# Attention and mixture-of-experts block: token lists by pair of experts written to DRAM sequence by sequence, an earlier table load, and products of the identity between the first transposes

## The chip, the cores and the metric

The kernel runs on one core of one Trainium2 chip. A time is the device time of one execution in microseconds (us). The figure that counts is the median of the runs; beside it one execution was taken by the hardware profiler, and its durations are those that the text works with. The core's engines are called PE (matrix products, with PEld for its weight loads), DVE (vector work), ACT (activations, copies), POOL (the general engine, which also issues indirect DMAs) and SP (which issues most DMAs).

## The reference, cut to what matters

The input is x, 16 sequences (B) of 512 tokens (S) of 256 numbers (D), in float32.

```
xn = layernorm(x)
q, k = elu(xn@Wq + bq) + 1, elu(xn@Wk + bk) + 1      # 16 heads of 16
v  = xn@Wv + bv
kv = sum over tokens of k (outer) v                  # per head
attn = (q @ kv) / max(q . sum(k), 1e-6) @ Wo + bo

shared = swiglu(xn@w_in.T) @ w_out.T                 # hidden 512
group  = argmax(softmax(xn@wg.T + gb))               # 2 groups of 4 experts
p      = softmax(expert logits within the group) * p_group
w_se   = the two largest p of a token, at their experts, else 0
h      = swiglu(xn@w1.T)
routed = sum over e of (h * w_se[:, e]) @ w2[e].T
out = x + attn + shared + routed
```

A token uses two of the four experts of one group, so there are 6 pairs in each group, 12 in all (`NP`). The 8192 tokens are sorted by pair, so that a tile of 128 tokens needs only the two weight matrices of its pair.

## The kernel before, in words

Tokens stand in 64 tiles of 128 (`TT`), four to a sequence (`NT`). The program has three stretches.

*The head.* `first` (L300 to L382) is written out by hand and pinned in program order: statistics of the first sequence's four tiles on DVE (`measure`, L320), square root on ACT (`scale`, L325), the normalised `xn` on DVE (L328), two transposes to a tile on PE (`place`, `pt`, L335), a copy back on ACT (L338), then the products for keys and router logits (`keys`, `pk`, L342) and for queries. The weights of the router (`we`, `wg`) and `wk` are loaded from ACT's queue (L143 to L145), ahead of the activation at L147 that brings in the square root's table. x is loaded from SP's queue (L110): the first sequence tile by tile, the next as a whole, and the third, `xs[2]`, last of the head's loads.

*The loop over sequences.* Each stage b makes the front of b+1 (residual L390, projections L412 and L423, feature map L397 to L402, routing L446 to L515), sums over b (`summarize` L689, `key_sum` of b+1 at L679), the attention's normaliser of b+1 (`attend`, L743 to L750, the chain through `rz`), the two hidden layers of b (`hidden_rows` L595 for the experts, `hidden` L621 for the shared part, both by a scheme of seven products for eight, whose sums and differences run on DVE at L574 to L584), the values (`pvk` L708, `vk` L717 and L722), their mixture with Wo (`pm` L731) and the outputs (`po` L768, in `gather`, which adds them to the residual at L777). Rows of 770 numbers (hidden state, residual and two weights) go to `h_d` in DRAM. Routing leaves two things for the sorting: `hot`, for each token a one-hot row of 12 over the pairs, and `ahead_of`, per partition a running count over tiles of the tokens of each pair (POOL, L515).

*The tiles.* With the tokens sorted, 75 tiles (`TILES`) are walked: the class `Tiles` gathers rows of `h_d` by indirect DMA (`rows`, L943, with the list `source`), transposes them (`turn`, L964 to L976), multiplies by two experts (`sums`, L993 to L1003) and scatters the result into the output (L1006, with the list `goal`). 67 tiles always run, the rest under a condition on `filled`.

Between loop and tiles stands `order` (L806 to L923), a generator. It is stepped by `between` from within `hidden_rows` and `gather` of the last two sequences. Its first part adds up the counts over partitions with two float32 products `pc` (L813, L815) and works out each token's slot among the sorted places. Then, for 8 groups of 8 tiles, `marks` makes one-hot rows of slot and tile on DVE (L877, L882, L886, L890) and `add` accumulates 64 bf16 products of them in `pi` (L894), which ends as a table of 128 places by 75 tiles with the number of the token in each. `source` and `goal` are read off it (L908 to L923).

The framework's scheduler sets the order on each engine, by priority and by what is ready, except where the kernel pins it. PSUM has two pools: `ps_mm` with six buffers and `ps_y` with two. SP issues its DMAs in program order[...].

Of the kernel before, what the change touches and what calls it, by code (L numbers as in the profile page):

```python
# [21 lines left out]
def block_kernel(  # L22
# [55 lines left out]
    TG = 8  # L78
    TR = 5
    assert TT % TG == 0  # L80
# [10 lines left out]

    h_d = dram.tile([TT * P, ROW], FP, name="h_d")

# [12 lines left out]
    def load_x(b, pieces=1):  # L106
        xt = x_all[:, b % 2]
        n = NT // pieces
        for i in range(pieces):
            tc.keep_in_program_order(nc.sync.dma_start(  # L110
                out=xt[:, ts(i, n), :], in_=x[b, ts(i, n * P), :].rearrange("(t p) d -> p t d", p=P)
            ))
        return xt
# [16 lines left out]
    xs = {0: load_x(0, NT)}  # L130
    KR = D + E + G
    wkr_sb = wp.tile([P, KD, KR], FP)

# [8 lines left out]

    nc.scalar.dma_start(out=wkr_sb[:, :, D : D + E], in_=we.rearrange("(p c) e -> p c e", p=P))  # L143
    nc.scalar.dma_start(out=wkr_sb[:, :, D + E : KR], in_=wg.rearrange("(p c) e -> p c e", p=P))
# [50 lines left out]
    def load_expert(i):  # L195
# [21 lines left out]
    before = const.tile([P, P], FP)  # L217
    nc.gpsimd.affine_select(
        out=before, in_=ones, pattern=[[1, P]],
# [4 lines left out]
    for j in range(EG):  # L224
        nc.gpsimd.memset(place[:, :, j : j + 1], float(j))
    BF = mybir.dt.bfloat16
    count = const.tile([P, P], BF)
    nc.gpsimd.iota(count, pattern=[[1, P]], base=0, channel_multiplier=0,
                   allow_small_or_imprecise_dtypes=True)
    number = const.tile([P, TT], BF)  # L230
    nc.gpsimd.iota(number, pattern=[[1, TT]], base=1, channel_multiplier=0,
                   allow_small_or_imprecise_dtypes=True)
    row = const.tile([P, 1], FP)
    nc.gpsimd.iota(row, pattern=[[0, 1]], base=0, channel_multiplier=1,
# [65 lines left out]
    def first():  # L300
# [57 lines left out]

        for t in range(NT):
            measure(0, t)  # L360
            scale(0, t, 1)
            if t:
                place(0, t - 1)
        keys(0)
# [152 lines left out]
    def between(b, n):  # L517

        if b + 2 >= B:
            for _ in range(n or 0):  # L520
                next(steps_of_order)
# [68 lines left out]
    def hidden_rows(b, xs7, then):  # L590

        rows = {}

        def product(to, u, i, start, stop):
            tc.keep_in_program_order(nc.tensor.matmul(  # L595
                to, lhsT=xs7[i][:, ts(u, P)], rhs=w1_in[W7[i]], start=start, stop=stop,
                skip_group_check=True,
            ))

        def room(u, half):  # L600
            rows[u, half] = work.tile([P, HID], FP, tag="hr", name=f"hr_{b}_{u}_{half}", bufs=4)
            return rows[u, half]

        def done(u, half, silu, product):
            nc.sync.dma_start(out=h_d[ts(b * NT + 2 * half + u, P), 0:HID], in_=rows[u, half])

        seven(f"phr_{b}", product, lambda a: a, room, done, lambda n: between(b, then(n)))
# [89 lines left out]
    def small_sums(b, shape, name):  # L697

        if b + 1 == B:
            return ps_y.tile(shape, FP, tag="py", name=f"{name}_{b}"), tc.keep_in_program_order  # L700
        return ps_mm.tile(shape, FP, tag="mm", name=f"{name}_{b}"), lambda step: step
# [25 lines left out]
    def mix(b, vk):  # L727
# [7 lines left out]
        with tc.high_priority() if b + 1 == B else nullcontext():  # L735
            nc.scalar.copy(kvo, pm)
# [22 lines left out]
    def outputs(b, t, qT, kvo, hs):  # L759
# [6 lines left out]
        parts += [(qT[:, c, ts(t, P)], kvo[:, c, :]) for c in range(KD)]  # L766
        for i, (a, w) in enumerate(parts):
# [3 lines left out]
    def gather(b, res, qT, kvo, hs, placed, then):  # L771

        for t in range(NT):
# [5 lines left out]
            between(b, then(t))  # L779
# [26 lines left out]
    def order():  # L806

        I32, U32 = mybir.dt.int32, mybir.dt.uint32
        total = keep.tile([P, NP], FP)
        nc.vector.tensor_copy(total, ahead_of[:, TT, :])  # L810
        pc = ps_mm.tile([P, 2 * NP], FP, tag="mm", name="pc")
        tc.keep_in_program_order(
            nc.tensor.matmul(pc[:, 0:NP], lhsT=before, rhs=total, start=True, stop=True)  # L813
        )
        nc.tensor.matmul(pc[:, NP:], lhsT=ones, rhs=total, start=True, stop=True)  # L815
        pcs = keep.tile([P, 2 * NP], FP)
# [3 lines left out]
        nc.vector.tensor_scalar(ci, pcs[:, NP:], float(P - 1), None, ALU.add)  # L820
# [5 lines left out]
        nc.vector.tensor_copy(runs[0][:, PAD:], ci)  # L826
        for i, d in enumerate((1, 2, 4, 8)):
# [3 lines left out]

        off = keep.tile([P, NP], FP)
        nc.vector.tensor_tensor(off, pcs[:, 0:NP], starts, ALU.add)
        sl = one.tile([P, TT, NP], FP, tag="low", name="sl")
        nc.vector.tensor_tensor(
            sl, ahead_of[:, 0:TT, :], off.unsqueeze(1).to_broadcast([P, TT, NP]), ALU.add
        )
        nc.vector.tensor_tensor(sl, sl, hot, ALU.mult)
        slot = keep.tile([P, TT], I32)
        slf = keep.tile([P, TT], FP)  # L840
        nc.vector.tensor_reduce(slf, sl, AX.X, ALU.add)
        nc.vector.tensor_copy(slot, slf)
        part = keep.tile([P, 2, TT], I32)
        nc.vector.tensor_scalar(part[:, 0, :], slot, P - 1, None, ALU.bitwise_and)
        nc.vector.tensor_scalar(part[:, 1, :], slot, 7, None, ALU.arith_shift_right)
        place_of = keep.tile([P, 2, TT], BF)
        nc.vector.tensor_copy(place_of, part)
# [12 lines left out]
        nc.vector.tensor_copy(where, of)  # L860
        yield


        pi = ps_y.tile([P, 2 * TILES], FP, tag="py", name="pi")

        los = x_all.rearrange("p b t d -> p (b t d)").bitcast(BF).rearrange("p (n t j) -> p n t j", t=TG, j=P)
        his = [
            a[:, B % 2].rearrange("p t d -> p (t d)").bitcast(BF)[:, 0 : TG * 2 * TILES].rearrange(
                "p (t i n) -> p t i n", t=TG, i=2
            )  # L870
            for a in (qq_all, kk_all, xn_all)
        ]

        def marks(g):
            row_of, tile_of = (place_of[:, i, ts(g, TG)].unsqueeze(2) for i in range(2))
            lo, hi = los[:, g % 4], his[g % 3]
            nc.vector.tensor_tensor(  # L877
                lo, count.unsqueeze(1).to_broadcast([P, TG, P]), row_of.to_broadcast([P, TG, P]),
                ALU.is_equal,
            )  # L880
            at_tile = one.tile([P, TG, TILES], BF, tag="at_tile", name=f"at_tile_{g}")
            nc.vector.tensor_tensor(  # L882
                at_tile, count[:, 0:TILES].unsqueeze(1).to_broadcast([P, TG, TILES]),
                tile_of.to_broadcast([P, TG, TILES]), ALU.is_equal,
            )
            nc.vector.tensor_tensor(  # L886
                hi[:, :, 0, :], at_tile,
                number[:, ts(g, TG)].unsqueeze(2).to_broadcast([P, TG, TILES]), ALU.mult,
            )
            nc.vector.tensor_scalar(hi[:, :, 1, :], at_tile, row, None, ALU.mult)  # L890

        def add(g):
            for t in range(TG):
                tc.keep_in_program_order(nc.tensor.matmul(  # L894
                    pi, lhsT=los[:, g % 4, t, :], rhs=his[g % 3][:, t].rearrange("p i n -> p (i n)"),
                    start=(g + t == 0), stop=(g * TG + t == TT - 1),
                ))


        for g in range(TT // TG + 2):  # L900
            if g > 1:
                add(g - 2)
                yield
            if g < TT // TG:
                marks(g)
                yield
        pis = keep.tile([P, 2, TILES], FP)
        nc.vector.tensor_copy(pis.rearrange("p i n -> p (i n)"), pi)  # L908
        free = keep.tile([P, TILES], FP)
        nc.vector.tensor_scalar(free, pis[:, 0, :], 0.0, float(2 * TT * P), ALU.is_equal, ALU.mult)  # L910
        tok = keep.tile([P, TILES], FP)
        nc.vector.scalar_tensor_tensor(
            tok, pis[:, 0, :], float(P), pis[:, 1, :], ALU.mult, ALU.add
        )
# [6 lines left out]
        nc.vector.tensor_scalar(source, tok, float(-P), 0.0, ALU.add, ALU.max)  # L921
        goal = keep.tile([P, TILES], U32)
        nc.vector.scalar_tensor_tensor(goal, tok, float(-P), free, ALU.add, ALU.add)  # L923
# [109 lines left out]
    xs[2] = load_x(2)  # L1033
    for b in range(B):
# [4 lines left out]
        if b + 2 == B:  # L1039
# [4 lines left out]
            steps_of_order = order()  # L1044
        if b + 1 == B:
            sums7 = token_sums(b, xnT)
            hidden_rows(b, sums7, {2: 2, 6: 2, 9: 2, 13: 2}.get)
# [3 lines left out]
            *lists, filled = next(steps_of_order)  # L1051
# [11 lines left out]
        elif b + 1 < B:  # L1063
            sums7 = token_sums(b, xnT)
            hidden_rows(b, sums7, {9: 1}.get)
# [5 lines left out]
        if b + 2 == B:  # L1071
            next(steps_of_order)
# [3 lines left out]
        if b + 1 < B:  # L1076
# [13 lines left out]
        if b + 2 == B:  # L1090
            next(steps_of_order)
# [5 lines left out]
        else:  # L1097
            gather(b, res, qT, kvo, hs, normed[b + 2][2]() if b + 2 < B else None, {0: 2, 1: 2, 3: 2}.get)
# [66 lines left out]
```

## Time and profile before

| | us |
|---|---|
| median of 3 runs | 1040.03 (1039.69 to 1040.49) |
| the profiled execution | 1033.23 |
| its span | 1031.5 |
| PE busy | 1004.9 (97%) |
| DVE busy | 779.4 (76%) |
| ACT busy | 488.1 (47%) |
| POOL busy | 254.8 (25%) |

The span is the time from the first to the last instruction that the profiler saw. An engine's busy time counts its instructions, not the time it stands before a semaphore. In a row of the timeline come start, duration, engine and line, operation, what is written and read, shapes, and in brackets the idle time before it with the instruction that ended that idle time. A row with x4 holds four instructions in sequence. The stage of one sequence takes some 46.5 us in the middle of the loop; the head ends, and the second sequence begins, near 74 us; the outputs of the last sequence end at 789.8, and after them come the tiles.

### The profile page before, as it was taken

Reading aid. Unit: us, or ns where it says so; the run is one execution under the profiler, and the core shown is the slowest. Engines: PE = TensorE matmul, PEld = TensorE weight load, DVE = VectorE, ACT = ScalarE, POOL = GpSimd, SP = SyncE. Lnnn points to the kernel's source line nnn. Section 1 sums busy time; section 2 is a strip of 40 time slices with the busy share of each in tenths; the row PEclk is TensorE's granted clock in tenths of the full one; section 3 lists DMA queues with packets and bytes.
Section 4 is the critical chain, followed back from the end, with each engine's and each line's share of the span. In section 5 each row is a group of like instructions: output and inputs, shape, how many; then the busy total and the mean of one; then the engine's idle time right before and its main releaser. Section 6 shows DMA issues by size and latency. Waiting matters only on the chain. (4 is left out here: it accounts for less than half of the span.)

```text
span 1031.5 us, 12407 instructions
## 1 busy us (share of the span) xinstructions
PE 1004.9 (97%) x3704; PEld 681.7 (66%) x3704; DVE 779.4 (76%) x1974; ACT 488.1 (47%) x893; POOL 254.8 (25%) x359
## 2 busy tenths in 40 slices
PE   7999999999999999999999999999899999999996
PEld 5466868677786868686777768686667344444442
DVE  5978687878778787878787877868975776666663
ACT  3525353535445253535343534425136576766671
POOL 5302020111202021110202020201012766555652
PEclk9999999999999999999999999999999999999999
DMA  7063534525152522314141313221235755555440
GB/s 220 16 177 107 141 104 101 147 59 154 51 163 54 161 84 81 122 42 143 37 128 56 110 55 123 72 77 61 62 110 146 225 172 153 147 156 157 150 147 30
DMA packets 130339, 116.08 MB, mean 113 GB/s; under 512 B 72637, under 2 KB 114109, under 8 KB 130272
## 3 DMA queue, kind: packets, MB, share of 16 engines
q1 hardware_dynamic: 120064, 77.43, 25.7%
q0 software_dynamic: 9392, 37.58, 12.2%
q8 instruction: 31, 0.51, 0.2%
q10 hardware_dynamic: 816, 0.27, 0.2%
q14 instruction: 36, 0.29, 0.1%
HBM read 65.36 MB, written 50.27 MB: 112 GB/s over the span
## 5 line engine op out<-in xcount | busy, mean ns | idle before, releaser
L993 PE MATMUL py<-w_sb,hT 128*128 x536 | 230.7, 592 | 1.7 <-DVE hT L976 1.6
L993 PEld LDWEIGHTS py<-w_sb,hT 128*128 128x128 f32 x536 | 101.7, 190 | 130.1 <-issue 129.1
L768 PE MATMUL po<-wout_sb,hs_all 128*128 128x256 f32 x480 | 116.6, 380 | 1.4 <-DVE hs_all L580 1.4
L390 POOL TENSOR_TENSOR res<-x_all,bo_sb 128x256 f32<-128x256 f32 x64 | 48.5, 792 | 274.4 <-DMA h_d<-res 203.4
L768 PEld LDWEIGHTS po<-wout_sb,hs_all 128*128 128x128 f32 x480 | 89.2, 190 | 15.1 <-DVE hs_all L580 3.4
L1006 POOL DMA_INDIRECT out<-y,goal x67 | 67.8, 1012 | 76.3 <-DVE y L1003 65.3
L676 POOL TENSOR_TENSOR k<-kk_all 128x512 f32<-128x512 f32 x16 | 20.9, 1307 | 258.3 <-DVE sm L458 247.7
L777 DVE TENSOR_TENSOR res<-po,res 128x256 f32<-128x256 f32 x60 | 25.4, 424 | 76.6 <-PE po L768 76.5
L398 ACT ACTIVATE km<-km 128x1024 f32<-128x1024 f32 x16 | 16.9, 1057 | 138.7 <-DVE km L397 134.4
L595 PE MATMUL phr_w<-w_sb,ss 128*128 128x512 f32 x120 | 61.5, 594 | 2.2 <-DVE ss L538 1.9
L768 PE MATMUL po<-kvo,qT 128*128 128x256 f32 x240 | 61.7, 383 | 0.0
L621 PE MATMUL phs_w<-ss,win_sb 128*128 128x256 f32 x240 | 61.6, 379 | 0.0
L621 PE MATMUL phs_t<-xnT,win_sb 128*128 128x256 f32 x240 | 61.6, 379 | 0.0
L595 PE MATMUL phr_t<-w_sb,xnT 128*128 128x512 f32 x120 | 61.3, 593 | 0.0
L595 PE MATMUL phr_t<-w_sb,ss 128*128 128x512 f32 x120 | 59.4, 597 | 0.0
L621 PE MATMUL phs_t<-ss,win_sb 128*128 128x256 f32 x240 | 59.1, 379 | 0.0
L689 PE MATMUL pxk<-kk_all,xn_all 128*128 128x256 f32 x256 | 58.0, 379 | 0.0
L412 PE MATMUL pk<-wkr_sb,xnT 128*128 128x266 f32 x240 | 57.2, 387 | 0.0
L423 PE MATMUL pq<-w_sb,xnT 128*128 128x256 f32 x240 | 54.2, 379 | 0.0
L689 PEld LDWEIGHTS pxk<-kk_all,xn_all 128*128 128x128 f32 x256 | 48.5, 190 | 6.7 <-issue 0.2
L964 ACT COPY hb<-qq_all 32x256 f32<-32x256 f32 x108 | 43.4, 402 | 17.1 <-DMA qq_all<-h_d,source 9.7
L412 PEld LDWEIGHTS pk<-wkr_sb,xnT 128*128 128x128 f32 x240 | 45.4, 190 | 8.0
(216 smaller groups left out, 1966.0 us busy)
## 6 DMA issues: line engine op xcount, KB each, us to landing
h_d<-hr SPq DMA_DIRECT2D x64, 256.0 KB, 2.5
q_d<-qq_all SPq DMA_DIRECT2D x16, 512.0 KB, 2.8
qb<-q_d SPq DMA_DIRECT2D x64, 128.0 KB, 3.1
w_sb<-in_w SPq DMA_DIRECT2D x64, 128.0 KB, 3.5
h_d<-res SPq DMA_DIRECT2D x60, 129.0 KB, 1.9
x_all<-in_x SPq DMA_DIRECT2D x15, 512.0 KB, 4.8
xn_d<-xn_all SPq DMA_DIRECT2D x14, 512.0 KB, 3.9
xb<-xn_d SPq DMA_DIRECT2D x56, 128.0 KB, 2.8
```

What stands on the lines that cost most here:

```text
L390: nc.gpsimd.tensor_tensor(res[:, t, 0:D], xt[:, t, :], bo_sb, ALU.add)
L412: nc.tensor.matmul(pk, lhsT=xnT[:, k, ts(t, P)], rhs=wkr_sb[:, k, :], start=(k == 0), stop=(k == KD - 1),)
L423: nc.tensor.matmul(pq[:, t, :], lhsT=xnT[:, k, ts(t2 + t, P)], rhs=wq_sb[:, k, :], start=(k == 0), stop=(k == KD - 1),)
L595: tc.keep_in_program_order(nc.tensor.matmul(to, lhsT=xs7[i][:, ts(u, P)], rhs=w1_in[W7[i]], start=start, stop=stop, skip_group_check=True,))
L621: tc.keep_in_program_order(nc.tensor.matmul(split(to)[:, f, :], lhsT=win_in[W7[i]][:, ts(2 * u + f, P)], rhs=xs7[i], start=start and f == ...
L676: nc.gpsimd.tensor_tensor(k2, kk[:, 0:2, :], kk[:, 2:4, :], ALU.add)
L689: nc.tensor.matmul(pxk[:, c, :], lhsT=xn[:, t, ts(c, P)], rhs=kk[:, t, :], start=(t == 0), stop=(t == NT - 1),)
L768: nc.tensor.matmul(po, lhsT=a, rhs=w, start=(i == 0), stop=(i == len(parts) - 1))
L777: nc.vector.tensor_tensor(res[:, t, 0:D], po, res[:, t, 0:D], ALU.add)
L964: nc.scalar.copy(there[ts(q, Q), a - near, 0:n, :], self.hg[ts(a, Q), 0:n, ts(q, W)])
L993: nc.tensor.matmul(py.rearrange("p j d -> p (j d)"), lhsT=self.hT[:, f, ts(j, P)], rhs=w2_sb[:, f, bass.ds(regs[i % TR], 2 * D)], start=(f ...
L1006: stored = nc.gpsimd.indirect_dma_start(out=out_rows, out_offset=bass.IndirectOffsetOnAxis(ap=self.goal[:, i : i + 1], axis=0), in_=y, in_ ...
```

## The change

Four parts.

1. *Lists by sequence.* After the routing of sequence b, `enlist(b)` works out the place of each of its 512 tokens within its pair: two bf16 products into `pr` (128x48), one of a triangular matrix with `hot`, one of ones with `ahead_of`; then four DVE operations, which add the start of the pair's list, mask, reduce to one number a token and tile, and turn it into an index `spot`. Four indirect DMAs from POOL write the tokens' numbers, 4 bytes each, into `lists_d` in DRAM, at a distance of 32 bytes. `clear_lists` first fills that array with a number that stands for "no token" (3.19 MB in seven DMAs from SP).
2. *`order`.* The one-hot groups, the 64 products and the slots are gone. One bf16 product `pc` gives the totals; a chain of small DVE operations gives, for each of the 75 tiles, the row of `lists_d` where it begins (`part`); one indirect DMA fetches those rows (`got`); a copy takes each eighth word (`tokens`), and a transposing product `pi` turns them into the layout of `source` and `goal`. It is no longer stepped from `hidden_rows` and `gather`; it starts after sequence 14's hidden layer. Within a list tokens now stand by tile and then by partition. An empty place gathers row 8191, where it was row 0, and is not scattered.
3. *Sequence 14.* Its values and mixture run within its hidden layer, as those of sequence 15 already did, and its outputs take the attention's part first.
4. *The head.* `we` and `wg` are loaded from SP's queue behind the second tile of x. Fifteen products of the identity with itself (`warm`) stand on PE: seven before the first transposes, two behind each of the first three pairs. Their result, `idle`, is not used.

The scheduler's order follows from these. On DVE in the head, the first statistics of the third sequence (L283, which need `xs[2]`) now stand ahead of five operations that stood before them: a first `ss`, two `ex`, and the additions of `kk_1_0` and its logits. In the loop, the pairs of `pr` products stand behind the key sums, and the four new DVE operations among the `rz` chain, ahead of the `hs` additions. The fifteen `idle` products, `pc` and `pi` use the pool `ps_y`.

The diff, cut to its core:

```diff
-    xs = {0: load_x(0, NT)}
+    def load_routers():
+        for w, at, n in ((we, D, E), (wg, D + E, G)):
+            tc.keep_in_program_order(nc.sync.dma_start(
+                out=wkr_sb[:, :, at : at + n], in_=w.rearrange("(p c) e -> p c e", p=P)
+            ))
+
+    xs = {0: load_x(0, NT, {1: load_routers})}
...
-    nc.scalar.dma_start(out=wkr_sb[:, :, D : D + E], in_=we.rearrange("(p c) e -> p c e", p=P))
-    nc.scalar.dma_start(out=wkr_sb[:, :, D + E : KR], in_=wg.rearrange("(p c) e -> p c e", p=P))
     nc.scalar.dma_start(out=wkr_sb[:, :, 0:D], in_=wk.rearrange("(p c) f -> p c f", p=P))
...
+        def warm(n):
+            for _ in range(n):
+                pin(nc.tensor.matmul(idle, lhsT=ident, rhs=ident, start=True, stop=True))
+
+        idle = ps_y.tile([P, P], FP, tag="py", name="idle")
+        warm(7)
         for t in range(NT):
             measure(0, t)
             scale(0, t, 1)
             if t:
                 place(0, t - 1)
+                warm(2)
...
+    def clear_lists():
+        free = work.tile([P, P * WORDS], U32, tag="blocks", name="free")
+        nc.gpsimd.memset(free, FREE)
+        R = lists_d.shape[0]
+        for r in range(0, R, P):
+            n = min(P, R - r)
+            nc.sync.dma_start(out=lists_d[r : r + n, :], in_=free[0:n, :])
...
+    def enlist(b):
+        pr = ps_y.tile([P, NT, NP], FP, tag="py", name=f"pr_{b}")
+        flat = pr.rearrange("p t c -> p (t c)")
+        mine = hot[:, ts(b, NT), :]
+        nc.tensor.matmul(flat, lhsT=before, rhs=mine.rearrange("p t c -> p (t c)"), start=True, stop=False)
+        nc.tensor.matmul(
+            flat, lhsT=ones_bf, rhs=ahead_of[:, ts(b, NT), :].rearrange("p t c -> p (t c)"),
+            start=False, stop=True,
+        )
+        rk = small.tile([P, NT, NP], FP, tag="rk", name=f"rk_{b}")
+        nc.vector.tensor_tensor(rk, pr, lists_at.unsqueeze(1).to_broadcast([P, NT, NP]), ALU.add)
+        nc.vector.tensor_tensor(rk, rk, mine, ALU.mult)
+        rf = small.tile([P, NT], FP, tag="rf", name=f"rf_{b}")
+        nc.vector.tensor_reduce(rf, rk, AX.X, ALU.add)
+        spot = small.tile([P, NT], U32, tag="spot", name=f"spot_{b}")
+        nc.vector.tensor_scalar(spot, rf, float(WORDS), None, ALU.mult)
+        for t in range(NT):
+            put = nc.gpsimd.indirect_dma_start(
+                out=entries,
+                out_offset=bass.IndirectOffsetOnAxis(ap=spot[:, t : t + 1], axis=0),
+                in_=ids[:, b * NT + t : b * NT + t + 1], in_offset=None,
+            )
+            tc.declare_no_dep(put.ins, group="lists", reason="every token has an entry of its own")
+            tc.add_to_no_dep_group("lists", put.ins)
...
-        if b + 1 == B:
+        if b + 2 >= B:
             return ps_y.tile(shape, FP, tag="py", name=f"{name}_{b}"), tc.keep_in_program_order
...
+        if b + 2 == B:
+            parts = parts[KH:] + parts[:KH]
...
     def order():
...
-        total = keep.tile([P, NP], FP)
-        nc.vector.tensor_copy(total, ahead_of[:, TT, :])
-        pc = ps_mm.tile([P, 2 * NP], FP, tag="mm", name="pc")
...
+        pc = ps_y.tile([P, NP], FP, tag="py", name="pc")
+        nc.tensor.matmul(pc, lhsT=ones_bf, rhs=ahead_of[:, TT, :], start=True, stop=True)
...
+        past = keep.tile([P, NP - 1], FP)
+        nc.vector.tensor_scalar(past, starts[:, 1:], row, None, ALU.is_le)
+        nc.vector.tensor_tensor(past, past, jump[:, 0 : NP - 1], ALU.mult)
+        begin = keep.tile([P, 1], FP)
+        nc.vector.tensor_reduce(begin, past, AX.X, ALU.add)
+        part = keep.tile([P, 1], U32)
+        nc.vector.tensor_scalar(part, begin, row, 1.0 / P, ALU.add, ALU.mult)
+        got = work.tile([P, P * WORDS], U32, tag="blocks", name="got")
+        nc.gpsimd.indirect_dma_start(
+            out=got[0:TILES, :], out_offset=None, in_=lists_d,
+            in_offset=bass.IndirectOffsetOnAxis(ap=part[0:TILES, :], axis=0),
+        )
+        tokens = keep.tile([P, P], FP)
+        nc.vector.tensor_copy(
+            tokens[0:TILES, :], got[0:TILES, :].rearrange("p (n w) -> p n w", w=WORDS)[:, :, 0]
+        )
         yield
-        pi = ps_y.tile([P, 2 * TILES], FP, tag="py", name="pi")
...
-        for g in range(TT // TG + 2):
-            if g > 1:
-                add(g - 2)
-                yield
-            if g < TT // TG:
-                marks(g)
-                yield
...
+        pi = ps_y.tile([P, TILES], FP, tag="py", name="pi")
+        nc.tensor.transpose(pi, tokens[0:TILES, :], ident[0:TILES, 0:TILES])
...
-        nc.vector.tensor_scalar(source, tok, float(-P), 0.0, ALU.add, ALU.max)
+        nc.vector.tensor_scalar(source, pi, float(TT * P - 1), None, ALU.min)
         goal = keep.tile([P, TILES], U32)
-        nc.vector.scalar_tensor_tensor(goal, tok, float(-P), free, ALU.add, ALU.add)
+        nc.vector.tensor_copy(goal, pi)
         yield source, goal, where, filled
...
     xs[2] = load_x(2)
+    clear_lists()
...
+        if b == 0:
+            enlist(0)
+        if b + 1 < B:
+            enlist(b + 1)
...
+            if b + 2 == B:
+                steps_of_order = order()
+                next(steps_of_order)
+            gather(b, res, qT, kvo, hs, normed[b + 2][2]() if b + 2 < B else None)
+            if b + 2 == B:
+                *lists, filled = next(steps_of_order)
```

## The prediction

> **What bounds the kernel now.** I read the busy shares first, then TensorE's waits, then the timeline of the stages that the change touches. From the page of the kernel before:
>
> ```profile
> span 1031.5 us, 12407 instructions
> PE 1004.9 (97%) x3704; PEld 681.7 (66%) x3704; DVE 779.4 (76%) x1974; ACT 488.1 (47%) x893; POOL 254.8 (25%) x359
> ...
> L1006 POOL DMA_INDIRECT out<-y,goal x67 | 67.8, 1012 | 76.3 <-DVE y L1003 65.3
> ```
>
> TensorE (PE) is busy for 97% of the span, so work taken off it, or a wait taken from it, shortens the span wherever PE sets the end. POOL is busy for a quarter. From TensorE's waits (for what: total, times, longest):
>
> ```profile
> PE pt L335 <- DVE xn_all L328: 7.5, 5, 5.3
> PE pm L731 <- DVE rz L748: 2.5, 1, 2.5
> PE phr_w L595 <- DVE ss L538: 1.9, 1, 1.9
> ...
> PE phs L663 <- DVE hr L651: 1.5, 1, 1.5
> ```
>
> The first is the start. The second and third belong to one place, the seam between sequence 14's stage and sequence 15's. Its timeline on PE (start, duration, operation; in brackets the idle time before it):
>
> ```profile
> 731.13 1.10 PE L731 MATMUL pm<-wo_sb,vk 128*128 128x256 f32 x4 [2.47 <-DVE rz L748]
> 735.49 0.69 PE L894 MATMUL pi<-qq_all,x_all 128*128 128x150 bf16 x8 [0.23 <-DVE qq_all L890]
> 738.22 0.59 PE L768 MATMUL po<-wout_sb,hs_all 128*128 128x256 f32 x2
> 738.65 0.70 PE L894 MATMUL pi<-kk_all,x_all 128*128 128x150 bf16 x8
> 739.19 1.50 PE L768 MATMUL po<-wout_sb,hs_all 128*128 128x256 f32 x6
> 744.52 1.06 PE L595 MATMUL phr_t<-w_sb,xnT 128*128 128x512 f32 x2
> 747.49 1.10 PE L595 MATMUL phr_w<-w_sb,ss 128*128 128x512 f32 x2 [1.91 <-DVE ss L538]
> ```
>
> The old list-building stands here: groups of one-hot comparisons (L877 to L890) keep DVE busy without a gap from 731 to 764.5, so `vk_14`, and then sequence 15's first sums, come late and PE waits. The x8 of the row at 738.65 takes up 0.54 us of PE (the next `po` starts at 739.19), 0.067 us a product.
>
> From there to the end it's PE again. The first row gathers start at 768.48, long before the first tile's product at 789.84, and the 24 products after it come every 0.43 us. A microsecond won near 735 reaches the end.
>
> In the head the bound changes hands:
>
> ```profile
> 8.97 1.98 PE L342 MATMUL pk<-wkr_sb,xnT 128*128 128x266 f32 x4
> 20.48 3.76 PE L412 MATMUL pk<-wkr_sb,xnT 128*128 128x266 f32 x16
> 24.78 0.43 DVE L283 BATCH_NORM_STATS2 st<-x_all 128x6 f32<-128x256 f32 x1 [2.48 <-DMA x_all<-in_x]
> 64.36 1.13 PE L731 MATMUL pm<-wo_sb,vk 128*128 128x256 f32 x4
> ```
>
> One size of product costs 0.49 us at 9 us and 0.235 us at 20 us: PE starts at half rate (the granted-clock column reads 1.00 in both, so only durations show it). DVE then stands 2.48 us for the third sequence's x, whose DMA the SP queue issues at 20.03. From 26.2 to 64 DVE has no idle time worth the name (29.87 of 30 us between 30 and 60), and `vk_0`, its last piece, ends at 64.31, just ahead of `pm`. So DVE's work behind 24.78 sets when PE leaves the first sequence.
>
> **Step 1, the old lists go (seam).** Removed from PE: 64 products of 0.067, 4.27 us; their wait, 0.2; the two fp32 products `pc` at 711, about 0.5; the waits for `vk` (2.47), for `ss` (1.91) and for `hr` (0.33), since what held DVE there, the marks, no longer exists. Sum 9.7 us off the path that sets the end.
>
> **Step 2, two `pr` products per sequence.** 32 bf16 products of 48 columns, each with a 128x128 weight load. Those of sequences 0 and 1 stand in the DVE-bound head; 28 stand in PE-bound stages. No row has their shape. Low end: two `pi` products with their loads, 0.13 us a pair. High end: the old `pc` pair (fp32, 12 columns), 0.25. They're bf16 like `pi`, but each change between fp32 and bf16 work leaves less to overlap, as at `pc`, so I take 0.2: 14 pairs, 2.8 us (1.8 to 3.5).
>
> **Step 3, lists by sequence on DVE and POOL.** DVE gets four small operations per sequence. By the nearest rows (L478 128x24 0.20, L510 reduction 0.19, L748 0.20) these are 0.7 to 0.8 us, behind `rz` (L743 to L750) and ahead of the `hs` additions. At 293.5 to 296.4 DVE waits 0.34, 0.44 and 0.42 us there, 1.2 in all, so this cover holds it: 0. Without the cover, 14 x 0.75 is 10.5 us. POOL gets 64 scatters of 128 entries of 4 bytes. By the L1006 row one costs POOL 1.01 us plus 0.30 between two, so 5.3 us per sequence of 46.5 on an engine that's three quarters idle. Queued behind them is only the next sequence's doubling of k (L676), some 10 us later. Nobody waits for the landing until the single gather `got` at the end: 0.
>
> A rule speaks against this step. The Trainium skill, "SBUF — State Buffer", section "Who interferes with whom", says that VectorE in a 2-port mode and GpSimd lock each other out for a whole instruction. The trace agrees that something of the kind exists: L467, 0.65 us usually, takes 1.02 while POOL runs L676. By the row of L943 (gathers of 0.95 to 1.04 us at 768 to 775, beside `vk` and `hs` operations at their usual 0.42 and 0.69) a scatter costs DVE nothing. By the rule a plain copy or tensor_scalar that meets one could wait up to about 1 us. Most operations near the scatters read two tensors or PSUM, so I go by the row and keep the rule for a rival.
>
> **Step 4, clearing the lists.** Seven SP DMAs, 3.19 MB, behind x[2]. SP issues nothing between 20.45 and 42.01, and at the 404 GB/s seen at 14 us they need 8 us: hidden, 0. Had they to share with the first q writes at 50, it would be up to 1 us.
>
> **Step 5, the new order at the seam.** A chain of some 16 small DVE operations starts after `phs_14` (about 728) and is interleaved with `hs` additions: about 6 us. Then one gather of 75 rows, 1 us of issue and 2.5 to 3.9 us to land (3.9 is the median of the row gathers), and a strided copy: tokens at 738 to 739.5. PE reaches the transposing product `pi` after four `po`, at about 739.1. So a wait of 0 to 2 us, taken as 0.5. Behind it on PE the whole of `phr_15` is queued. `pi` itself 0.3 and `pc` 0.1.
>
> **Step 6, the head.** The router weights move from ACT's queue to SP's, so ACT's table load (2.81, 1.28 us) starts 1.3 us earlier and the first `xn` (4.72) comes some 0.5 us earlier. Fifteen identity products keep PE at work before its first need. Cold `pk` records cost 4 x 0.255 + 5 x 0.19 = 1.9 us more than warm ones. The Trainium skill, "TensorE: Matmul & The Clock Gate", Part 1 (the HAM clock gate), says full rate comes after about 3.4 us of sustained work; with products from 2.6 us it would be there by 9, and all 1.9 us would go. By the trace, PE began at 5.28, worked in snatches, and was fast only at 13.2, 8 us later; from 2.6 that gives 10.6, and perhaps 1.2 of it goes. By neither is it worth anything at the end, since what follows still meets the wait for x[2] at 24.78. That load is issued behind two more SP DMAs (0.63 each): 0 to 1.3 later, taken as 0.6. And the new DVE order puts its statistics ahead of five operations which used to fill time before the wait (a first `ss`, 0.33; two `ex`, 0.18; `kk_1_0`, 0.33; `lg`, 0.10), so 0.94 us lands behind it, and eight list operations of sequences 0 and 1 add 0.9. Head: +2.4 us, from 0 to +4.
>
> **Sum.** -9.7 + 2.8 + 0.5 + 0.4 + 2.4 = -3.6. The profiled execution took 1033.23 (span 1031.5 and 1.7 around it), so 1029.6. The runs' median is 1040.03, 6.8 above it; carried along, the forecast is 1036.4.
>
> **Rivals.** B, full gain: the head is neutral because the ACT and clock gains carry through, and `pr` costs its low end. Then -9.7 + 1.8 + 0.9 to -7 or more, with a PE start that gains 1 to 2 it's -8.5: about 1031.5. For it: PE-bound stages have no other limit. Against it: the DVE stretch from 26 to 64.
>
> C, nothing measurable (0.2%, 2.1 us, is about what a measurement of this kernel can tell from no change): the token chain is 2 us late, the head +4, `pr` 3.5: -9.7 + 3.5 + 2.4 + 4 = +0.2, with milder terms about -0.5, so 1039.5. For it: three waits each have a cause ahead of them.
>
> D, slower: the scatters hold DVE, by the port rule. Place: between `rz` and the `hs` additions in each of 14 sequences. Cover there is 1.2 us, of which the list operations use 0.75, so a hold shows from 0.45 us per sequence and outweighs the 3.6 from 0.7. One hold of 1 us gives 14 x 0.55 - 3.6 = +4: 1044; two give 14 x 1.55 - 3.6 = +18: 1058. Against it: the L943 row.
>
> **How the numbers follow.** Forecast 0.45, B 0.2, C 0.15, D 0.2. The forecast's own range is 1033 to 1038.5. The range must hold C and the mild end of D: 1031 to 1044. Faster by over 0.2% (below 1038): B and most of the forecast, 0.6. Same: C and the forecast's upper end, 0.19. Slower: D and a little of C, 0.21.
>
> **What would show it.** PE's waits no longer list `pm` for DVE at 731 nor `phr_w` for `ss`; `phr_15` starts about 9 us sooner against `phs_14`'s end. DVE's `rz` and `hs` rows keep their means (1.22, 0.69). `pr` pairs stand 0.13 to 0.25 us apart. `pm_0` starts at 66 to 67 rather than 64.36; if it starts at or before 64, B holds. If the stretch from one sequence to the next grows beyond 46.5 us plus 0.2, D holds. The forecast is wrong above all if tokens come after 741, or if a stage that was PE-bound gains a wait on DVE.

## The result, and the profile after

The changed kernel is slower: 1045.79 us (median, 1044.67 to 1046.42) against 1040.03, a ratio of 1.0051 (95% interval 1.004 to 1.0062). The forecast was 1036.4, so it has the wrong sign. The changed kernel's page:

```profile
span 1044.7 us, 12545 instructions
PE 1009.7 (97%) x3696; PEld 685.3 (66%) x3696; DVE 756.2 (72%) x2000; ACT 487.8 (47%) x893; POOL 330.4 (32%) x426
...
L568 POOL DMA_INDIRECT lists_d<-ids,spot x64 | 74.2, 1160 | 184.4 <-DVE spot L566 158.0
L1008 POOL DMA_INDIRECT out<-y,goal x67 | 68.0, 1015 | 82.7 <-DVE y L1005 72.1
```

DVE has 23 us less to do, POOL 76 more, and the span is longer. TensorE's waits in the changed kernel (for what: total, times, longest):

```profile
PE py L995 <- DVE hT L978: 5.2, 1, 5.2
PE pr L555 <- DVE ksb L735: 5.1, 1, 5.1
PE idle L375 <- POOL ident masks.py:199: 2.6, 1, 2.6
PE pt L348 <- DVE xn_all L341: 2.4, 1, 2.4
PE pxk L743 <- DVE sm L479: 1.5, 1, 1.5
```

The waits of the seam (`pm` for `rz`, `phr_w` for `ss`) are gone, as forecast. In their place stands one at 52 us that no step of the forecast held: `pr` waiting for the copy of a key sum. The first row, among the tiles, isn't the change's: a second trace of the kernel before has it too, with 4.7 us. Of the traces behind this text some have one such wait of 4.5 to 5.2 us and tiles of 239 to 240 us, the others only short ones (at most 2.4 us) and tiles of 233 to 235 us, whichever kernel it is. The kernel before ran in 1040 us in most groups of runs and in 1033 in one, and the traces of that group all lack the wait; what decides it was not found. So below a time is compared with the kernel before run beside it, and stages with the second trace of before, which has the wait. By stages, in us:

| stage | before, second trace | changed | difference | forecast |
|---|---|---|---|---|
| head, to the first key product of sequence 2 | 73.74 | 82.81 | +9.1 | +2.4 |
| 13 stages, to the same of sequence 15 | 618.1 | 619.5 | +1.4 | +2.6 |
| seam and last sequence, to the first tile's product | 98.5 | 87.3 | -11.2 | -8.6 |
| tiles, to the last scatter | 239.6 | 239.9 | +0.3 | 0 |
| after the last scatter | 8.0 | 15.2 | +7.3 | 0 |
| span | 1037.9 | 1044.7 | +6.8 | -3.6 |

So the gain is there, and more than its size; it is lost again at two places, in the head and behind the last instruction that computes anything. The head of the changed kernel, on TensorE and with one row of DVE (the copy `ksb`):

```profile
48.46 0.19 PE L555 MATMUL pr<-hot,before 128*128 128x48 bf16 x1
48.49 0.18 PE L556 MATMUL pr<-ahead_of,ones_bf 128*128 128x48 bf16 x1
...
50.43 1.02 PE L717 MATMUL phs<-xnT,w_sb 128*128 128x512 f32 x2
51.29 1.02 PE L717 MATMUL phs<-xnT,win_sb 128*128 128x512 f32 x2
56.92 0.41 DVE L735 COPY ksb<-pks 128x256 f32<-128x256 f32 x1
57.39 0.20 PE L555 MATMUL pr<-hot,before 128*128 128x48 bf16 x1 [5.07 <-DVE ksb L735]
57.41 0.21 PE L556 MATMUL pr<-ahead_of,ones_bf 128*128 128x48 bf16 x1
57.45 3.76 PE L717 MATMUL phs<-xnT,win_sb 128*128 128x512 f32 x4
61.00 1.91 PE L717 MATMUL phs<-xnT,w_sb 128*128 128x512 f32 x2
62.71 2.90 PE L717 MATMUL phs<-xnT,win_sb 128*128 128x512 f32 x6
```

The second `pr` waits 5.07 us, and behind the wait a `phs` product takes 0.89 us from start to start (four from 57.45 to 61.00), where it took 0.43 ahead of it (two from 50.43 to 51.29): TensorE has fallen back to half rate. The granted clock is 0.50 from 57.4 to 62.7 and 1.00 ahead of the wait. The six products take 5.26 us instead of 2.58, so 2.7 us more. The Trainium skill ("TensorE: Matmul & The Clock Gate", Part 1) has the clock halved after an idle window of about 3.4 us, until about as long a stretch of sustained work. This wait fits the first half of that; the slow stretch behind it is longer, 5.3 us. And 3.4 us is no sharp bound here: in the seam of the second trace of before, a wait of 2.48 us was enough (granted clock 0.61 behind it), and in the first trace one of 2.47 was not (1.00).

And the end. POOL's last drain, in the rows of the program's closing line, of the second trace of before and of the changed kernel (durations in ns, shortest, median and longest, then first and last start in us):

```profile
L1161 POOLq DRAIN  x3: 51/103/3418, 1033.6 to 1037.6; - x3
```

```profile
L1167 POOLq DRAIN  x3: 51/103/8727, 1035.1 to 1044.4; - x3
```

The long one is 3.418 us before and 8.727 after. The last instructions of the other engines come only when it is done.

### The profile page after: what moved, and what is told of

Read it like the earlier page. It is cut to its first block, busy times and chain, and to the rows that moved or that the text cites. A ratio compares the mean times of both kernels' runs of the same rounds, so it can differ in the third digit from the quotient of the medians.

```text
span 1044.7 us, 12545 instructions
## 1 busy us (share of the span) xinstructions
PE 1009.7 (97%) x3696; PEld 685.3 (66%) x3696; DVE 756.2 (72%) x2000; ACT 487.8 (47%) x893; POOL 330.4 (32%) x426
## 4 chain that ended last, share of the span: by engine, by line
PE 81%; DVE 9%; DMA 3%; issue 3%; ACT 1%; SPq 1%; another core or an unknown queue 1%; POOL 0%; POOLq 0%; DVEq 0%; ACTq 0%
PE py L995 20%; PE po L824 14%; PE phr_t L649 9%; PE phs_t L675 7%; PE pk L433 5%; PE pxk L743 5%; PE pq L444 5%; PE phr_w L649 4%; PE phs_w L675 3%; PE phr_l L649 2%; PE phs_l L675 2%; PE pm L785 1%; PE phs L717 1%; DMA x_all<-in_x 1%; DMA w_sb<-in_w 1%
## 5 line engine op out<-in xcount | busy, mean ns | idle before, releaser
L568 POOL DMA_INDIRECT lists_d<-ids,spot x64 | 74.2, 1160 | 184.4 <-DVE spot L566 158.0
L419 ACT ACTIVATE km<-km 128x1024 f32<-128x1024 f32 x16 | 16.9, 1058 | 140.9 <-DVE km L418 136.6
```

The costliest lines, as they stand in the source:

```text
L568: put = nc.gpsimd.indirect_dma_start(out=entries, out_offset=bass.IndirectOffsetOnAxis(ap=spot[:, t : t + 1], axis=0), in_=ids[:, b * NT + ...
```

## The experiments

### Second traces

Both kernels unchanged.

> The kernel before, unchanged, for a second trace. The first profiled execution (1033.2 us) lies 6.8 under the median of the runs (1040.0). Theory A, that it was a lucky execution: this one takes about 1040, and the 7 us show as one more stall among the tiles or as a later end of TensorE's sequencer after the last product. Theory B, that the profiler itself shortens it: again 1033.

> The changed kernel, unchanged, for a second trace. Its first trace reaches the first tile's product at 789.57 (before: 789.84) and then loses 13 us: 5.2 in one wait near 818, 2 at half clock behind it, and 7 after the last scatter. Theory A, that these come from the new order of tokens in the lists: the same wait at the same tile. Theory B, that they are how executions fall: another place or none, and a time anywhere from 1037 to 1046.

Before: 1039.65 us, span 1037.9, with a wait of 4.73 us for `hT` at 819 to 824, and a last drain of 3.418 us as in the first trace. Changed: 1044.88, span 1043.2, the same wait (4.67), drain 8.727 again, and the wait for `ksb` (3.5 us). Theory A of the first holds as to the wait, and not as to the end, which is the same in both traces of before. Of the second, both theories fall: the wait among the tiles is in both kernels, and the long end is not how an execution falls; it is in every trace of the changed kernel. The stages repeat well: the 13 stages took 618.1 us in both traces of before and 619.5 in both of the changed kernel.

### The list of sequence 0 made one stage later

Key sums and `pr` both take their PSUM buffers from `ps_y`, which has two. In stage 0 the key sum of sequence 1 holds one, the first `pr` gets the other, and the second must wait until DVE has copied the key sum out.

```diff
-        if b == 0:
-            enlist(0)
         if b + 1 < B:
             enlist(b + 1)
...
+            if b == 1:
+                enlist(0)
             if b + 2 == B:
                 steps_of_order = order()
```

> The changed kernel with the list of sequence 0 made in stage 1 instead of stage 0, so that the second PSUM pool's two buffers hold key sums 1 and one list product, not two. Theory A, that the second pr product waited 5.07 us for a buffer (until VectorE had copied key sum 1) and threw the clock back to half rate: the wait at 52 to 57 is gone, the second sequence's first keys start at 74 to 76 rather than 80.1, and the time falls by 4 to 6 us. Rival, that VectorE sets the end of the first sequence anyway: the wait moves to the mixture pm, and the time falls by less than 2.

1040.4 us beside 1040.03 for before: ratio 1.0004 (0.9995 to 1.0013), some 5 us under the changed kernel. The head of this kernel on TensorE:

```profile
47.62 0.19 PE L555 MATMUL pr<-hot,before 128*128 128x48 bf16 x1
48.37 0.18 PE L556 MATMUL pr<-ahead_of,ones_bf 128*128 128x48 bf16 x1 [0.56 <-POOL ahead_of L536]
...
51.12 2.74 PE L717 MATMUL phs<-xnT,win_sb 128*128 128x512 f32 x6
...
66.71 1.10 PE L785 MATMUL pm<-wo_sb,vk 128*128 128x256 f32 x4 [0.92 <-issue]
...
76.28 3.76 PE L433 MATMUL pk<-wkr_sb,xnT 128*128 128x266 f32 x16
```

The wait for `ksb` is gone and so is the half rate behind it (one of 0.56 us for the counts is left), and the first key product of sequence 2 starts at 76.28 instead of 82.81 (81.64 in the second trace of the changed kernel). Theory A holds. What is left is VectorE's again: `vk_0` ends at 66.61, and `pm` starts at 66.71, 2.35 to 2.57 us later than in the two traces of before.

### The head undone

```diff
-    xs = {0: load_x(0, NT, {1: load_routers})}
+    xs = {0: load_x(0, NT)}
...
+    nc.scalar.dma_start(out=wkr_sb[:, :, D : D + E], in_=we.rearrange("(p c) e -> p c e", p=P))
+    nc.scalar.dma_start(out=wkr_sb[:, :, D + E : KR], in_=wg.rearrange("(p c) e -> p c e", p=P))
...
-        warm(7)
...
-                warm(2)
```

> The changed kernel with the head undone: router weights on ACT's queue, no products of the identity. Theory A, that the two loads ahead of x tiles 3 and 4 and of the third sequence's x cost some 2 us at the wait for that x: the statistics of the third sequence start at 24.8 rather than 26.7, and the time falls by about 2. Rival, that the clock and table gains pay for it: the time rises by 0 to 2.

1043.21 us, ratio 1.0031 (1.0019 to 1.0042): some 2 us better than the changed kernel. But the statistics of the third sequence start at 26.54, no earlier than with the new head (26.67). The size came out as theory A had it and its mechanism didn't: the two loads are not what delays that x. This kernel keeps the wait for `ksb`, with 3.45 us, and its sequence 2 starts at 80.64, so part of its gain is a shorter wait and not the head undone. What the two loads do delay shows on DVE in the changed kernel:

```profile
5.79 0.41 DVE L341 TENSOR_SCALAR xn_all<-x_all,mv,rs 128x256 f32<-128x256 f32 x1
9.26 0.43 DVE L333 BATCH_NORM_STATS2 st<-x_all 128x6 f32<-128x256 f32 x1 [3.06 <-DMA x_all<-in_x]
```

DVE has to wait for the third tile of x until 9.26, where in the kernel before it takes that tile at 6.58 without a wait, so TensorE stands for 2.4 us after its products of the identity and starts its first keys at 11.72, at half rate again:

```profile
11.27 0.61 PE L375 MATMUL idle<-ident 128*128 128x128 f32 x4
11.72 1.87 PE L355 MATMUL pk<-wkr_sb,xnT 128*128 128x266 f32 x4
```

### POOL's last drain: more transfers

Twice the scatters, the second set into a DRAM array that nobody reads; then, in the kernel before, 64 plain transfers of one element; then half as many more scatters.

```diff
+        for t in range(NT):
+            put = nc.gpsimd.indirect_dma_start(
+                out=spare,
+                out_offset=bass.IndirectOffsetOnAxis(ap=spot[:, t : t + 1], axis=0),
+                in_=ids[:, b * NT + t : b * NT + t + 1], in_offset=None,
+            )
```

> The changed kernel with every list scatter made twice, the second into a DRAM array that nobody reads: 64 more indirect DMAs of 128 entries from POOL. Theory A, that POOL's last drain grows with what its queue has issued: before 3.418 us, changed 8.727, so 64 more add another 5.3 to about 14.0, and the time from the last scatter to the end of the span grows from 15.0 to 20 or more. Rival, that the longer drain belongs to something else in the change (the gather of the lists, the 4-byte entries landing late): 8.7 again. The scatters themselves stay hidden in either case.

```diff
         route(b, lg, res)
+        for i in range(NT):
+            nc.gpsimd.dma_start(out=spare_d[b * NT + i : b * NT + i + 1, 0:1], in_=row[0:1, 0:1])
```

> The kernel before, with 64 plain one-element DMAs from POOL added, four per sequence. If the drain goes by the number of DMAs (5.31 us over 65, 0.082 each), it is 8.7 us here and the time from the last scatter to the end grows from 7.0 to about 14; if it goes by entries, or by the indirect kind alone, it stays near 3.4.

```diff
-        for t in range(NT):
+        for t in range(2):
             put = nc.gpsimd.indirect_dma_start(
                 out=spare,
```

> The changed kernel with 32 more scatters (two per sequence, into an array that nobody reads), between the changed kernel's 64 and the 128 of the doubled one, whose last drain was 8.727 and 5.215 us. If the drain goes by where a ring of fixed length stands at the end, this one is anywhere between 2.8 and 12; if it has to do with the amount, it is about 7. Either way it is not a cost per scatter.

Each of these three ran once. The doubled kernel's drain is not 14 but 5.215 us, and it runs in 1033.7 us beside 1033.34 for before, so relative to before it is faster than the change with half its scatters. The plain transfers raise the drain of before to 7.252 (1041.78 beside 1033.34; its head is longer too, by some 4 us, and its 13 stages are not, 618.1). With half as many more it is 2.677, the shortest of all. That kernel's time, 1038.81 beside 1040.48, says little: its trace lacks the long wait among the tiles (234.7 us), and its 13 stages are longer by some 5 us (TensorE waits for `vk` at six of the mixtures, 3.9 us in all), whose cause is open.

```profile
L1177 POOLq DRAIN  x3: 51/103/5215, 1025.9 to 1031.6; - x3
```

```profile
L1164 POOLq DRAIN  x3: 51/103/7252, 1031.6 to 1039.4; - x3
```

```profile
L1177 POOLq DRAIN  x3: 51/103/2677, 1033.6 to 1036.8; - x3
```

The first is the doubled kernel's, the second that of the plain transfers, the third that with half as many more. A price per transfer is out:

| kernel | transfers from POOL beyond before's | last drain, us | last scatter to end, us |
|---|---|---|---|
| before | 0 | 3.4 | 8.0 |
| tiny_dmas | 64, plain | 7.3 | 12.5 |
| changed | 65 | 8.7 | 15.2 |
| half_more | 97 | 2.7 | 7.8 |
| twice | 129 | 5.2 | 10.1 |

The idea in half_more's expectation, a ring whose position at the end decides, isn't contradicted by this, but no run shows it. What sets the length of the drain was not found.

### POOL's last drain: one more drain

If the last drain works off something left over, an earlier drain could do that where POOL is idle.

```diff
         if b + 1 < B:
             enlist(b + 1)
+        if b + 2 == B:
+            tc.keep_in_program_order(nc.gpsimd.drain())
```

With the list of sequence 0 in stage 1 (mid_drain), and in the changed kernel itself (drain_alone), which ran beside a third run of the changed kernel.

> pr0_late (list of sequence 0 made in stage 1) with one more drain of POOL, placed behind the last list scatter and ahead of the first row gathers, where POOL is idle. If a drain only has to work through what was issued since the last one, the mid one takes some 5 us beside other work, the last one falls from 8.7 to about 3.4, and the time falls by about 5 us from 1040.4 to 1035. If the last drain goes by all that was ever issued, it stays 8.7 and the time stays.

> The changed kernel again, as the reference of this call's chip (the two chips seen so far differ by some 6 us among the tiles, for the kernel before and the changed one alike). Ratio to before 1.004 to 1.006, last drain of POOL 8.7 us.

> The changed kernel with the one more drain of POOL behind the last list scatter, and nothing else (sequence 0's list in stage 0 as in the change). Theory A, that the end costs 7 us because the last drain is long: it falls from 8.7 to about 2.8, the stretch from the last scatter to the end from 15 to 8, and the time by 7 us against the changed kernel of this call. Rival, that the mid drain's gain came from the lists being made later: less than 2 us.

The changed kernel beside it: 1045.36 us, ratio 1.0047 (1.0032 to 1.0062), drain 8.727. With the one drain: 1037.4, ratio 0.9971 (0.9962 to 0.9981), 8 us faster, its last drain:

```profile
L1169 POOLq DRAIN  x3: 51/103/2824, 1032.9 to 1036.3; - x3
```

From the last scatter to the end it has 7.7 us, against 15.2 in the changed kernel's trace beside it, while head, stages, seam and tiles of the two agree within 0.4 us each. Without the PSUM wait as well (mid_drain): 1027.67 beside 1033.34, ratio 0.9946 (0.9929 to 0.9962). There the drain in the middle lasts 11.0 us from 727.2, through the four last list scatters:

```profile
L1075 POOLq DRAIN  x1: 11041/11041/11041, 727.2 to 727.2; - x1
```

The gather of the lists follows at 739.97, 7.8 us after the last of those scatters, when its index `part` is ready. So theory A holds with its numbers: the long end goes with the last drain, and an earlier drain removes it. Why the change's drain is long at all stays open.

The kernel before, with a drain ahead of its first row gathers:

```diff
         if b + 1 == B:
+            tc.keep_in_program_order(nc.gpsimd.drain())
             for w in tiles[:AHEAD]:
                 w.rows()
```

> The kernel before with one drain of POOL ahead of the first row gathers. If the mid drain takes something off the last one that every kernel has, the last one falls from 3.4 to 2.8, the time by 0.6 us or not measurably; the change's own lists then keep their whole gain of about 8 us against it.

1039.68 beside 1040.48, ratio 0.9991 (0.9984 to 0.9998); drain 2.832, which is 0.6 us shorter. The kernel before has little to gain from one more drain.

### What the head still loses

> pr0_late with the clearing of the lists held back: its fill is worked out from the third sequence's x, so that its seven DMAs can't start before that x has landed. Theory A, that the 3.2 MB shared the DMA engines with that x and made it land 1 to 2 us later: the statistics of the third sequence start near 24.8 rather than 25.8, and the time falls by 1 to 2 us. Rival, that the two router loads ahead of it in the queue are the delay: nothing changes.

```diff
-        nc.gpsimd.memset(free, FREE)
+        nc.gpsimd.tensor_scalar(
+            free, xs[2].rearrange("p t d -> p (t d)"), 0.0, float(FREE), ALU.mult, ALU.add
+        )
```

1034.42 beside 1033.34, ratio 1.0011 (1.0004 to 1.0018), statistics at 26.71: no gain. Its x was issued late (21.00), and its new fill on POOL ran beside DVE's work. From its timeline:

```profile
26.77 1.04 POOL L540 TENSOR_SCALAR free<-x_all 128x1024 uint32<-128x1024 f32 x1 [7.74 <-DMA x_all<-in_x]
...
27.05 0.80 DVE L470 TENSOR_TENSOR ex<-lg,mx 128x32 f32<-128x32 f32 x1
```

`ex` takes 0.17 to 0.18 us in the other traces and ends here with POOL's fill. So it settled nothing. Three kernels with both repairs (the list of sequence 0 in stage 1, the drain behind the last list scatter) take it up: best_oldhead undoes the head as above, best_warm undoes only the router loads and keeps the products of the identity, and best_clear is best_oldhead with the clearing held back by a fill on ACT:

```diff
-        nc.gpsimd.memset(free, FREE)
+        nc.scalar.activation(
+            free, xs[2].rearrange("p t d -> p (t d)"), AF.Copy, bias=float(FREE), scale=0.0
+        )
```

> Sequence 0's list in stage 1, the drain behind the last list scatter, and the head undone (router weights on ACT's queue, no products of the identity). If the new head costs what it cost beside the stall (2.6 us), the ratio to before falls from 0.9946 to about 0.992. If what it lost was only the earlier start of that stall, it stays at 0.9946.

> The same, but with the products of the identity kept and only the router weights back on ACT's queue. Theory A, that the loads ahead of the third x tile are the cost and the products worth nothing at the end: the same time as without them, within 0.5 us, although the first keys' products run at full rate. Rival, that the clock's gain gets through: 1 to 2 us faster.

> The kernel of best_oldhead with the clearing held back behind the third sequence's x, its fill made on ScalarE instead of POOL so that nothing meets VectorE's port. Theory A, that the 3.2 MB of the clearing are what makes that x land 1.5 to 2 us later: the third sequence's statistics start near 24.7 rather than 26.6, pm_0 near 64.8 rather than 66.6, and the ratio to before is 0.9905 to 0.9915. Rival: they start at 26 or later and the ratio stays at 0.9924.

best_oldhead: 1032.37 beside 1040.13, ratio 0.9924 (0.991 to 0.9937). best_warm: 1033.5, 0.9936 (0.9923 to 0.995), not distinguishable from it, nor from mid_drain, which has the whole new head (0.9929 to 0.9962). With the router weights off SP's queue the products do what they can do. From best_warm's timelines:

```profile
9.36 1.06 PE L357 MATMUL pk<-wkr_sb,xnT 128*128 128x266 f32 x4
10.53 2.86 PE L357 MATMUL pk<-wkr_sb,xnT 128*128 128x266 f32 x12
...
25.70 0.43 DVE L298 BATCH_NORM_STATS2 st<-x_all 128x6 f32<-128x256 f32 x1 [5.46 <-DMA x_all<-in_x]
26.04 0.17 DVE L472 TENSOR_TENSOR ex<-lg,mx 128x32 f32<-128x32 f32 x1
...
66.59 1.10 PE L787 MATMUL pm<-wo_sb,vk 128*128 128x256 f32 x4 [0.76 <-issue]
```

The first keys are at full rate, and the last query product ends near 16.9 rather than 18.3 as in the first trace of before. Then DVE waits 5.46 us for the third sequence's x, and `pm` starts at 66.59, where it starts without the products too (66.56 in best_oldhead). That these two agree is a cancellation: the x of best_warm is there 0.9 us sooner (25.70 against 26.61), but with the products the five DVE operations stand behind the wait (`ex` at 26.04), and without them they fill it (`ex` at 22.17). From 28.01 on both run alike.

best_clear: 1031.27 beside 1040.48, ratio 0.9907 (0.989 to 0.9923). Its x lands 4.9 us after its issue at 20.70, against 6.2 in best_oldhead (issued at 20.42, seen by DVE at 26.61); in the second trace of before it was 4.4. The statistics start at 25.59 and `pm` at 65.80, 0.76 us sooner. Over all traces, from issue to statistics it's 5.7 to 6.7 us in the eleven that issue the clearing right behind that x and 4.4 to 4.9 in five that don't, on average 6.1 and 4.6. So the clearing's traffic very likely costs that x some 1.5 us; against it stands clear_late, which took 5.7 without it. Whether the later clearing gains time is not shown: the ratios of best_clear and best_oldhead overlap, and `pm` at 65.80 isn't far from the 66.56 to 67.38 of the other repaired kernels with the early clearing.

## Why the prediction was wrong, point by point

Between the -3.6 us forecast and the +6.8 measured lie 10.4. The head has 6.7 of them and the end 7.3; the seam and the 13 stages came out 3.8 better than forecast.

- *Step 1, the seam.* Right in mechanism; the stretch gained 11.2 us against the second trace of before (10.5 against the first), where steps 1 and 5 with `pr` came to 8.6. The rows give the difference. Each group of eight `pi` took 0.53 to 0.54 us of TensorE, as costed, and TensorE stands nowhere in the changed seam. In the second trace of before the wait for `rz` brought half rate too:

```profile
730.95 1.10 PE L731 MATMUL pm<-wo_sb,vk 128*128 128x256 f32 x4 [2.48 <-DVE rz L748]
731.89 3.17 PE L768 MATMUL po<-wout_sb,hs_all 128*128 128x256 f32 x8
734.85 1.48 PE L768 MATMUL po<-kvo,qT 128*128 128x256 f32 x4
```

Those twelve `po` took 4.28 us to the next row at 736.17, where they take 2.59 at full rate (732.07 to 734.66 in the first trace). So 1.7 us is a price of the old wait that I costed at nothing. The rest is small: `pr`, `pc` and the new `pi` cost 0.4 instead of 0.6, the wait for `tokens` that was taken as 0.5 is not in the trace compared, and the first products behind each old wait took up to 0.2 longer.
- *Step 2, `pr`.* 1.35 us over 13 stages, 0.10 a pair, where the range was 0.13 to 0.25; the `pi` row was the nearer, and going towards the fp32 row of `pc` was wrong. And its price was asked only of TensorE's time. **The first step that failed is here: I did not count the buffers.** "Those of sequences 0 and 1 stand in the DVE-bound head" took their place for harmless and put their cost at nothing, but in stage 0 three tiles (`pks_1` and two `pr`) want the two buffers of `ps_y`. TensorE waited 5.07 us there with the rest of `phs_0` queued behind it, and ran the next six products at half rate. It cost 5 us (pr0_late).
- *Step 3, lists on DVE and POOL.* DVE's rows stood (85 to 690 us): `qk` 1.218 and the sum `rz` 1.220 us against 1.217 and 1.220, `hs_all` 0.688 as before. A scatter occupies POOL 1.16 us (forecast 1.01) and holds nobody. Rival D is refuted by the +0.1 us per stage, and the row of L943 was the right one to go by: a computing instruction of POOL held DVE up (`ex` in clear_late, 0.80 us instead of 0.17 to 0.18), these scatters did not. **The second step that failed is the "0" for POOL:** "nobody waits for the landing" was true, but I looked only at who waits inside the program. At its end POOL's last drain is 5.3 us longer, with some 2 us more between the last scatter and its start. drain_alone took 8 us off with one earlier drain. That the scatters alone lengthen the drain is not shown (with twice as many it is shorter), only that the changed kernel's drain is long.
- *Step 4, the clearing.* Its cover, an empty SP queue, was real, but the 3.2 MB started right behind the third sequence's x. The traces make this some 1.5 us of that x's delay, with clear_late against it.
- *Step 5, the new order.* `pi` waits at most 0.5 us for `tokens` (0.3 in the second trace), as taken.
- *Step 6, the head.* Without the PSUM wait the head costs +2.3 to +3.2 us (76.28 in pr0_late and 76.95 in mid_drain against 73.74 to 73.96), about the size forecast, and by luck: the make-up is another. The x of the third sequence comes 1.0 to 2.1 us late (I took 0.6), and four of the eight list operations are not in these heads any more. The 0.94 us of the five operations came as forecast (best_warm against best_oldhead). The third tile of the first sequence comes 2.0 to 2.8 us late behind the router weights, which I had not costed, but that ends in the wait for x[2], as does the clock's gain (best_warm; there full rate was in place for the first keys at 9.36, as the first of my two estimates had it).
- *Rivals and chances.* Slower had 0.21, for a mechanism that didn't occur. Neither of the two that did was among the rivals.

## What to carry to other kernels

Before a new PSUM tile is called cheap, count the tiles of its pool that are alive at each place where the product stands, and ask which copy frees the buffer it gets: here two buffers and three tiles turned 0.1 us of products into 5. The stretch behind the last computing instruction belongs to the kernel's time; with transfers from POOL look at its last drain, and if it is long, put one more drain where POOL has time. Both repairs turn the change's 1.0051 into 0.9946; with the old head and a later clearing it was 0.9907, a difference of which the traces explain less than half. And a long wait of TensorE costs more than itself, since the products behind it can run at half rate (2.7 us here, 1.7 in the old seam).

## What the runs showed of the hardware

POOL's last drain took from 2.68 to 8.73 us, the same to 0.01 us in each trace of one kernel wherever that was looked at twice (3.418 in two traces of before, 8.727 to 8.731 in six traces of four kernels with the change's transfers and no drain between), and it neither rises nor falls with the number of transfers alone. An extra drain leaves 2.82 to 2.83 at the end, whichever kernel it stands in. Two small loads (8 and 2 KB) ahead of a tile of x in one queue moved its statistics by 2.0 to 2.8 us (8.56 to 9.41 in the traces with them there, 6.58 in best_warm, which has them on the other queue), though their issue takes 1.3. TensorE was at half rate behind waits of 5.07 and 3.48 us, and behind waits of 2.48 us in two traces but not in two others (2.47 and 2.48), at the same place of nearly the same kernel.
